# A four-layer graph network: layer 2 in units of up to three chunks, and the last group's tiles not cleared

## The chip, the cores and the metric

The kernel runs on one core of a Trainium2 chip. The metric is device time in microseconds. Before the change it is 1073.04 us, the median of three runs (1072.29 to 1073.3).

## The reference

There are 3327 nodes with 512 features, and a sparse adjacency matrix of 3327 x 3327 integers with some four neighbours a row. Four layers follow each other, each with a layer norm and a ReLU ahead and a residual around it:

```python
h = jnp.maximum(_layernorm(x, axis=-1), 0.0)
x = x + _L0_gnn_ref(h, adj, ...)   # mean over neighbours, two projections, a third on both, ReLU
h = jnp.maximum(_layernorm(x, axis=-1), 0.0)
x = x + _L1_gnn_ref(h, adj, ...)   # graph attention, 8 heads of 64
h = jnp.maximum(_layernorm(x, axis=-1), 0.0)
x = x + _L2_gnn_ref(h, adj, ...)   # graph attention, 4 heads of 128, quaternion weights, ELU
h = jnp.maximum(_layernorm(x, axis=-1), 0.0)
x = x + _L3_gnn_ref(h, adj, ...)   # graph attention, 1 head of 512
```

An attention layer projects every node to `Wh`, scores each edge by `leaky_relu(f_src[i] + f_dst[j])`, takes the softmax over the neighbours of a node, and sums the neighbours' `Wh` rows with those weights.

## The kernel before

The nodes are padded by one to 3328 and cut into 26 chunks of 128 rows. Everything that a layer needs of other nodes it gathers by index.

A first stage reads `adj` and `x`. For each chunk, `look` (L1189) loads two halves of the adjacency rows as integer tiles `ai` (four buffers) through `bring_rows` (L1182). VectorE finds the places of ones (`max_index`, L1209) and ScalarE counts them (L1217). The last chunk, number 25, has 127 rows, so `start` (L1197) clears the tile with a GpSimd memset (L1200) before its load, and `start_x` (L1289) clears its `x` tile with a VectorE memset (L1292). The loads of a chunk are issued on SyncE's queue, in the order in which the program emits them, and one that waits for a cleared tile holds those behind it. The same stage computes layer 0's projections on TensorE (L1349), makes the neighbour lists, and sorts the nodes by degree. Each node's row is then scattered to its sorted place in `own` (L1435).

After the sort, chunk 0 holds the nodes of highest degree. A chunk has as many slots as its largest degree can be: chunks 0 to 25 have 14, 8, 7, 7, 6, 6, 6, 5, 5, 5, 5, then five chunks of 4 (11 to 15), five of 3 (16 to 20), three of 2 (21 to 23) and two of 1. That makes 117 gathers a layer. One gather is an indirect DMA on GpSimd's queue (L1562): 128 rows of about 2 KB from the layer's `table` in DRAM into one of 33 places of the tile `ring`. `gather` (L1545) gives a chunk consecutive places, and starts from place 0 where the rest does not hold it. A place is written again once the chunk that held it has been read.

A layer's work on a chunk (`attend`, L1911) is: gather the slots; scores, softmax and weights on VectorE and ScalarE (L1941 to L1978), once for all chunks of a *unit*; scale the rows by the weights (VectorE L2110, ScalarE L2096 for one row in five); sum them in PSUM on TensorE with an identity matrix (`sum_on_pe`, L1593); in layer 2 the ELU, with the tiles `neg` and `ee` (L2164, L2166); add to the residual `xres` (L2178). Then `project` (L1602) makes the next layer's table: statistics for each chunk (L1649), the inverse deviation for the unit at once (`rough` L818, `refined` L827), ReLU, four transposes, a copy with sums, the products with the next layer's weights (L1737 for layer 3), and a store to the table on SyncE's queue (L1764). In layer 3 the weighted rows are summed on VectorE into a tile `y` (L2030), which TensorE transposes (L2046) and multiplies (L2060).

No layer's gather may start before the whole table is written: the `mark` memset (L2194) on GpSimd waits for all its stores.

The order of all this comes from `Plan` (L614). Every step is added with an engine, a cost and a rank, and with what it takes and gives of the limited buffers (`limits`, L1524). `Plan.run` (L650) goes through a schedule in which the step that can start first goes first, ties by rank, and emits the steps in that order; so a unit's place in `ORDERS` (L578) sets its rank, and its size and the number of buffers shape the order of instructions on every engine. Costs of the memsets are not among the plan's.

Of the kernel before, what the change touches and what calls it, by code (L numbers as in the profile page):

```python
# [8 lines left out]
F32 = mybir.dt.float32  # L9
# [9 lines left out]
P = 128  # L19
# [7 lines left out]
def general_path(  # L27
# [519 lines left out]
    def l3_finish(pc, i, o):  # L547
# [37 lines left out]
        (8, 13), (6,), (1,), (0,), (3,), (25,),  # L585
    ),
    2: (
        (18, 23), (19, 24), (16,), (20,), (6, 11), (10, 14), (7, 12), (5, 13), (9,), (1,), (21, 22), (4,), (0,),
        (8,), (2,), (3,), (15,), (17,), (25,),
    ),  # L590
    3: (
        (0,), (7,), (17,), (15, 20), (25,), (11,), (3,), (23,), (1, 5), (24,), (4, 14), (16,), (12, 22), (8,),
# [100 lines left out]
def gnn_stack_kernel(  # L693
# [19 lines left out]
    nc = tc.nc  # L713
    N, D = x_in.shape
    NK = (N + P - 1) // P
    NP = NK * P
    LAST = N - (NK - 1) * P
# [17 lines left out]
    with ExitStack() as st:  # L735
# [82 lines left out]
        def rough(pool, tag, var, scale=1.0):  # L818

            n = var.shape[-1]  # L820
            ln = pool.tile([P, 2], F32, tag="ln", name=f"ln{tag}", bufs=3)[:, :n]
            nc.scalar.activation(ln, var, AF.Ln, bias=eps, scale=scale)
            r0 = pool.tile([P, 2], F32, tag="r0", name=f"r0{tag}", bufs=3)[:, :n]
            nc.scalar.activation(r0, ln, AF.Exp, bias=lift, scale=-0.5)
            return r0

        def refined(pool, tag, mv, r0):  # L827

            n = r0.shape[-1]
            a = pool.tile([P, 2], F32, tag="nra", name=f"nra{tag}", bufs=3)[:, :n]  # L830
            nc.vector.scalar_tensor_tensor(a, r0, -1.0, r0, ALU.mult, ALU.mult)
            nc.vector.scalar_tensor_tensor(a, mv[:, :, 1], EPS, a, ALU.add, ALU.mult)
            r = pool.tile([P, 2], F32, tag="rs", name=f"rs{tag}", bufs=3)[:, :n]
            nc.vector.scalar_tensor_tensor(r, a, 3.0 * LIFT * LIFT, r0, ALU.add, ALU.mult)
            nmr = pool.tile([P, 2], F32, tag="nmr", name=f"nmr{tag}", bufs=3)[:, :n]
            nc.vector.scalar_tensor_tensor(nmr, mv[:, :, 0], -1.0, r, ALU.mult, ALU.mult)
            return r, nmr

        def refined_sums(pool, tag, mv, r0):

            n = r0.shape[-1]
            a = pool.tile([P, 2], F32, tag="nra", name=f"nra{tag}", bufs=3)[:, :n]
            nc.vector.scalar_tensor_tensor(a, r0, -1.0 / D, r0, ALU.mult, ALU.mult)
            nc.vector.scalar_tensor_tensor(a, mv[:, :, 1], D * EPS, a, ALU.add, ALU.mult)
            r = pool.tile([P, 2], F32, tag="rs", name=f"rs{tag}", bufs=3)[:, :n]
            nc.vector.scalar_tensor_tensor(r, a, 3.0 * LIFT * LIFT, r0, ALU.add, ALU.mult)
            nmr = pool.tile([P, 2], F32, tag="nmr", name=f"nmr{tag}", bufs=3)[:, :n]
            nc.vector.tensor_tensor(nmr, mv[:, :, 0], r, ALU.mult)
            return r, nmr


        with tc.tile_pool(name="p0", bufs=1) as pa, tc.tile_pool(name="p0p", bufs=2, space=PSUM) as pp:
# [329 lines left out]
            def bring_rows(dst, src, i):  # L1182
                if i < NK - 1:
                    nc.sync.dma_start(dst, src[i * P : (i + 1) * P, :])
                else:
                    nc.sync.dma_start(dst[:cut, :], src[i * P : i * P + cut, :])
                    nc.sync.dma_start(dst[cut:LAST, :], src[i * P + cut : N, :])

            def look(pos, i):  # L1189

                found = []
                rank = (ADJ * pos, 0)
                for hf in range(2):
                    key = f"{i}_{hf}"
                    cols = min(HW, N - hf * HW)

                    def start(i=i, hf=hf, key=key, cols=cols):  # L1197
                        ai = new("ai", key, [P, HW], I32)
                        if i == NK - 1:
                            nc.gpsimd.memset(ai, 0)  # L1200
                        bring_rows(ai[:, :cols], adj[:, hf * HW : hf * HW + cols], i)

                    o = load(rank, 4.0 * P * HW, start, take=("ai",), lag=1.6)

                    def find(i=i, hf=hf, key=key, cols=cols):
                        ai = tiles["ai", key]
                        for q in range(SEG // 2):
                            qq = hf * (SEG // 2) + q
                            nc.vector.max_index(  # L1209
                                fidx[:, i, qq * 8 : (qq + 1) * 8], one_i, ai[:, q * QW : min(cols, (q + 1) * QW)]  # L1210
                            )

                    a = put("dve", 2.06, rank, find, (), [o])

                    def square(i=i, hf=hf, key=key, cols=cols):
                        junk = pa.tile([P, HW], I8, tag="junk", name=f"junk{key}")
                        nc.scalar.activation(  # L1217
                            junk[:, :cols], tiles["ai", key][:, :cols], AF.Square, accum_out=sq[:, i, hf : hf + 1]
                        )

                    b = put("act", 1.8, rank, square, (), [o])
                    plan.add("none", 0.0, rank, None, [a, b], give=("ai",))
                    found.append(a)
                return found
# [63 lines left out]

            def start_x(i):  # L1289
                x = node(i)[:, :D]  # L1290
                if i == NK - 1:
                    nc.vector.memset(x, 0.0)  # L1292
                bring_rows(x, x_in, i)

            own_done = {}
# [220 lines left out]
        with tc.tile_pool(name="run", bufs=1, reuse_waits="tile") as pr, tc.tile_pool(  # L1516
# [4 lines left out]
            hsum = {  # L1521
                layer: pr.tile([P, NK, DC], F32, tag=f"hsum{layer}", name=f"hsum{layer}") for layer in (1, 2, 3)
            }
            limits = {"xy": 3, "acc": 2, "pt": 2, "pw": 2, "h": 3, "hT": 3, "t": 3, "neg": 2, "ee": 2, "y": 3}  # L1524
            limits.update({"norm": 2, "soft": 2, "w": 3, "mv": 3})
            plan = Plan(limits)
            tiles = {}
# [74 lines left out]
            def project(layer, unit, updated, rank):  # L1602
# [6 lines left out]
                n = len(unit)  # L1609
                norm = {}  # L1610
                seen = []
                if SUMMED[layer]:


                    def emit():
                        m = tiles["mv", (layer, unit[0])]
                        nc.vector.tensor_scalar(m[:, :n, 0], m[:, :n, 0], -1.0 / D, None, ALU.mult)

                    centred = plan.add("dve", 0.17, rank, emit, updated)
                    for j, i in enumerate(unit):  # L1620
# [12 lines left out]

                    guessed = plan.add("act", 0.6, rank, emit, seen)

                    def emit():
                        norm["r"], norm["nmr"] = refined_sums(
                            pr, f"{layer}_{unit[0]}", tiles["mv", (layer, unit[0])][:, :n, :], norm["r0"]
                        )

                    normed = plan.add("dve", 0.8, rank, emit, [guessed], take=("norm",), give=("mv",))
                else:
                    for j, i in enumerate(unit):

                        def emit(j=j, i=i):
                            if j == 0:
                                norm["mv"] = new("mv", (layer, unit[0]), [P, 2, 2])
                            st6 = pr.tile([P, 6], F32, tag="st6", name=f"st6_{layer}_{i}", bufs=2)
                            nc.vector.bn_stats(st6, xres[:, i, :])  # L1649
                            nc.vector.bn_aggr(norm["mv"][:, j, :], st6)  # L1650

                        seen.append(
                            plan.add("dve", 0.88, rank, emit, [updated[j]] + seen, take=("mv",) if j == 0 else ())
                        )

                    def emit():
                        norm["r0"] = rough(pr, f"{layer}_{unit[0]}", norm["mv"][:, :n, 1])

                    guessed = plan.add("act", 0.6, rank, emit, seen)

                    def emit():
                        norm["r"], norm["nmr"] = refined(
                            pr, f"{layer}_{unit[0]}", norm["mv"][:, :n, :], norm["r0"]
                        )

                    normed = plan.add("dve", 0.8, rank, emit, [guessed], take=("norm",), give=("mv",))
# [169 lines left out]
            def summing(layer, unit, j):  # L1836

                if not SUMMED[layer]:
                    return {}
                if j == 0:  # L1840
                    new("mv", (layer, unit[0]), [P, 2, 2])
                return {"accum_out": tiles["mv", (layer, unit[0])][:, j, 0:1]}


# [415 lines left out]
```

## Time and profile before

| | us |
|---|---|
| median of the runs | 1073.04 |
| the profiled execution's own time | 1231.77 |
| its span | 1230.0 |
| first stage and layer 0, to the first mark | 514.2 |
| layer 1, mark to mark | 245.3 |
| layer 2, mark to mark | 239.0 |
| layer 3, to the end | 231.5 |

The mean granted TensorE clock was 0.855 of full speed. Over the span TensorE was busy 901.8 us, VectorE 726.6, ScalarE 518.2 and GpSimd 610.1. In layer 2 they were busy 172.0, 151.5, 110.6 and 134.1 us. The profiled execution took 158.7 us longer than the median run, so its spans serve for proportions and for the durations of instructions, and differences of stages are compared only between profiles. In the views PE is TensorE, PEld its weight loads, DVE VectorE, ACT ScalarE, POOL GpSimd and SP SyncE; a `q` behind a name is that engine's sequencer. A timeline line has the start, the time taken, the engine, the line of the kernel, the operation, what it writes and reads, and in brackets the idle time before it and what ended it. "issue" and "remote" there name no instruction of another engine that was waited for.

### The profile page before, as it was taken

How to read it: one execution, taken by the hardware profiler on the slowest of the kernel's cores; microseconds unless marked ns; L12 is line 12 of the kernel's file. 1: busy time of each engine (PE TensorE's matmuls, PEld its weight loads, DVE VectorE, ACT ScalarE, POOL GpSimd, SP SyncE). 2: the span in 40 equal slices, each digit the busy share in tenths (PEclk: the TensorE clock that was granted, in tenths of full speed). 3: DMA queues.
4: the chain of work that ended last, by engine and by line, in shares of the span. 5: the costliest groups of instructions: out<-in, count | busy, mean ns of one | idle time of the engine just before them, and what ended most of it. 6: DMA issues, size and time to landing. Idle time of an engine off the chain costs nothing. (4 is left out here: it accounts for less than half of the span.)

```text
span 1230.0 us, 11605 instructions
## 1 busy us (share of the span) xinstructions
PE 901.8 (73%) x2853; PEld 510.4 (41%) x2853; DVE 726.6 (59%) x1848; ACT 518.2 (42%) x1700; POOL 610.1 (50%) x719
## 2 busy tenths in 40 slices
PE   7599999854098889752979796539979832948865
PEld 4244444322075656531647464214435421423322
DVE  6499989204176557453869784628894815534441
ACT  4488886210043433422656553316554621312221
POOL 1064246717655550175757511766883236675661
PEclk9899999977599899966989889659896956978987
DMA  9999894958587772265666521665754345575561
GB/s 352 338 364 338 294 306 146 317 203 286 172 268 252 247 249 89 76 195 149 198 183 178 154 79 55 189 187 150 209 169 129 91 121 149 168 206 160 163 186 59
DMA packets 89910, 240.49 MB, mean 196 GB/s; under 512 B 24933, under 2 KB 26477, under 8 KB 89834
## 3 DMA queue, kind: packets, MB, share of 16 engines
q0 software_dynamic: 41600, 137.72, 38.1%
q1 hardware_dynamic: 48234, 101.96, 23.3%
q8 instruction: 24, 0.39, 0.1%
q14 instruction: 52, 0.43, 0.1%
HBM read 190.35 MB, written 49.27 MB: 195 GB/s over the span
## 5 line engine op out<-in xcount | busy, mean ns | idle before, releaser
L1562 POOL DMA_INDIRECT ring<-table,nbr x351 | 368.5, 1050 | 185.5 <-issue 80.9
L1593 PE MATMUL acc<-ring,ident 128*128 128x512 f32 (+1 forms) x494 | 266.6, 676 | 66.8 <-DVE ring L2110 24.3
L1780 PE MATMUL pw<-w,hT 128*128 128x264 f32 (+1 forms) x832 | 197.3, 394 | 18.3 <-ACT hT L1705 13.6
L1780 PEld LDWEIGHTS pw<-w,hT 128*128 128x128 f32 x832 | 161.2, 195 | 60.9 <-ACT hT L1705 20.5
L1593 PEld LDWEIGHTS acc<-ring,ident 128*128 128x128 f32 (+1 forms) x494 | 98.7, 215 | 175.1 <-issue 107.5
L1562 POOL DMA_INDIRECT ring<-table,srec x117 | 110.1, 941 | 77.8 <-issue 31.5
L2110 DVE TENSOR_TENSOR ring<-ring,w 128x2048 f32<-128x2048 f32 (+7 forms) x76 | 114.3, 1531 | 4.7 <-DVE w L1978 3.0
L2060 PE MATMUL pw<-w,hT 128*128 128x512 f32 x208 | 101.7, 634 | 13.3 <-ACT hT L2052 11.0
L1209 DVE FIND_INDEX8 fidx<-one_i,ai 128x8 uint32<-128x832 int32 x104 | 104.2, 1018 | 0.0
L1349 PE MATMUL pz_n<-wf,hT_n 128*128 128x512 f32 x208 | 95.2, 609 | 10.9 <-ACT hT_n L1342 8.4
L1705 ACT ACTIVATE hT<-pt 128x128 f32<-128x128 f32 (+1 forms) x312 | 81.8, 292 | 39.7 <-PE pt L1694 18.5
L1217 ACT ACTIVATE junk<-ai 128x1664 int8<-128x1664 int32 (+1 forms) x52 | 82.7, 1590 | 32.6 <-DMA ai<-in_adj_dram 32.2
L1694 PE MATMUL pt<-ident,h 128*128 128x128 f32 x208 | 36.5, 312 | 75.9 <-ACT h L1676 73.4
L1349 PE MATMUL py_n<-wf,hT_n 128*128 128x512 f32 x208 | 91.9, 592 | 0.0
L1803 ACT COPY t<-pw 128x512 f32<-128x512 f32 (+1 forms) x54 | 30.6, 566 | 134.0 <-PE pw L1780 43.9
L1941 DVE TENSOR_TENSOR e<-ring,fs 128x24 f32<-128x24 f32 (+25 forms) x96 | 15.2, 172 | 120.2 <-DMA ring<-table,nbr 102.0
L2060 PEld LDWEIGHTS pw<-w,hT 128*128 128x128 f32 x208 | 42.3, 207 | 73.2 <-issue 51.3
L1705 ACT ACTIVATION_READ_ACCUMULATOR hT<-pt 128x1 f32 x312 | 69.5, 223 | 0.0
L1694 PEld LDWEIGHTS pt<-ident,h 128*128 128x128 f32 x208 | 28.1, 160 | 96.3 <-ACT h L1676 81.6
L2194 POOL MEMSET mark<- 1x1 f32 x3 | 0.3, 88 | 132.7 <-DMA table<-t 132.7
L1349 PEld LDWEIGHTS pz_n<-wf,hT_n 128*128 128x128 f32 x208 | 39.8, 195 | 62.8 <-issue 49.4
L2046 PE MATMUL pt<-ident,y 128*128 128x128 f32 x96 | 16.4, 312 | 67.4 <-issue 56.8
(185 smaller groups left out, 1319.7 us busy)
## 6 DMA issues: line engine op xcount, KB each, us to landing
ai<-in_adj_dram SPq DMA_DIRECT2D x25, 832.0 KB
ai<-in_adj_dram SPq DMA_DIRECT2D x25, 831.5 KB
table<-t SPq DMA_DIRECT2D x52, 258.0 KB
xy<-own SPq DMA_DIRECT2D x26, 512.0 KB
table<-t SPq DMA_DIRECT2D x26, 260.0 KB
table<-zt_n SPq DMA_DIRECT2D x26, 256.0 KB
ring<-table,nbr POOLq DMA_INDIRECT x351
later<-in_x_dram SPq DMA_DIRECT2D x15, 256.0 KB
```

Of the source, the lines that this page charges most:

```text
L1209: nc.vector.max_index(fidx[:, i, qq * 8 : (qq + 1) * 8], one_i, ai[:, q * QW : min(cols, (q + 1) * QW)])
L1217: nc.scalar.activation(junk[:, :cols], tiles["ai", key][:, :cols], AF.Square, accum_out=sq[:, i, hf : hf + 1])
L1349: nc.tensor.matmul(pz, tiles["hT", key][:, c, :], wf[s][:, c, :], start=(c == 0), stop=(c == DC - 1))
L1562: nc.gpsimd.indirect_dma_start(out=ring[:m, r0 + s, : width[layer]], out_offset=None, in_=table[layer], in_offset=bass.IndirectOffsetOnAxi ...
L1593: nc.tensor.matmul(acc, ident[:m, :], g[:m, s, :D], start=(k == 0), stop=(k == len(slots) - 1))
L1694: nc.tensor.transpose(pt[:, c, :], h[:, c * P : (c + 1) * P], ident)
L1705: nc.scalar.activation(hT[:, c, :n], pt[:, c, :n], AF.Copy, accum_out=hsum[layer][:, i, c : c + 1])
L1780: nc.tensor.matmul(pw[:, b, :w], tiles["hT", key][:, c, :], wsb[layer][:, c, b, :w], start=(c == 0), stop=(c == DC - 1),)
L1803: nc.scalar.copy(t[:, :D].rearrange("p (b f) -> p b f", b=2)[:, lo:hi, :], pw[:, lo:hi, :HD])
L2046: nc.tensor.transpose(pt[:, c, :], tiles["y", key][:, c * P : (c + 1) * P], ident)
L2060: nc.tensor.matmul(pw[:, 0, :], tiles["hT", key][:, c, :], w3[:, c, :], start=False, stop=(c == DC - 1))
L2110: nc.vector.tensor_tensor(v, v, box["w"][:m, j, lo:hi, :].unsqueeze(3).to_broadcast([m, hi - lo, H, O]), ALU.mult,)
```

## The change

Layer 2's 26 chunks are taken in 18 units instead of 19, in another order; two units have three chunks, where the largest had two. The small tiles that hold one value per chunk of a unit are three wide instead of two. Of the tiles `neg` and `y` there is one buffer less each. The adjacency and feature tiles of the last chunk are no longer cleared: `bring_rows` loads the last real row once more into the one padding row, a third DMA for each of the three tiles. Later steps leave the padding node out by `real` (L781) and by the bounds of the output's scatter, as they did.

```diff
     2: (
-        (18, 23), (19, 24), (16,), (20,), (6, 11), (10, 14), (7, 12), (5, 13), (9,), (1,), (21, 22), (4,), (0,),
-        (8,), (2,), (3,), (15,), (17,), (25,),
+        (21,), (16, 24), (22,), (9, 17, 19), (12,), (2,), (23,), (11, 14), (15, 20), (5,), (4, 7, 13), (6, 8),
+        (0,), (1,), (3,), (18,), (10,), (25,),
     ),
...
-            ln = pool.tile([P, 2], F32, tag="ln", name=f"ln{tag}", bufs=3)[:, :n]
+            ln = pool.tile([P, 3], F32, tag="ln", name=f"ln{tag}", bufs=3)[:, :n]
...
                     nc.sync.dma_start(dst[:cut, :], src[i * P : i * P + cut, :])
                     nc.sync.dma_start(dst[cut:LAST, :], src[i * P + cut : N, :])
 
+                    nc.sync.dma_start(dst[LAST:P, :], src[N - 1 : N, :])
+
...
                         ai = new("ai", key, [P, HW], I32)
-                        if i == NK - 1:
-                            nc.gpsimd.memset(ai, 0)
                         bring_rows(ai[:, :cols], adj[:, hf * HW : hf * HW + cols], i)
...
                 x = node(i)[:, :D]
-                if i == NK - 1:
-                    nc.vector.memset(x, 0.0)
                 bring_rows(x, x_in, i)
...
-            limits = {"xy": 3, "acc": 2, "pt": 2, "pw": 2, "h": 3, "hT": 3, "t": 3, "neg": 2, "ee": 2, "y": 3}
+            limits = {"xy": 3, "acc": 2, "pt": 2, "pw": 2, "h": 3, "hT": 3, "t": 3, "neg": 1, "ee": 2, "y": 2}
...
-                                norm["mv"] = new("mv", (layer, unit[0]), [P, 2, 2])
+                                norm["mv"] = new("mv", (layer, unit[0]), [P, 3, 2])
```

The other tiles of `rough`, `refined` and `refined_sums` and the other `mv` change in the same way as `ln` and `mv`.

More of the change, by code (lines that the diff above doesn't have):

```diff
@@ L820, in rough @@
             n = var.shape[-1]
-            ln = pool.tile([P, 2], F32, tag="ln", name=f"ln{tag}", bufs=3)[:, :n]
+            ln = pool.tile([P, 3], F32, tag="ln", name=f"ln{tag}", bufs=3)[:, :n]
             nc.scalar.activation(ln, var, AF.Ln, bias=eps, scale=scale)
-            r0 = pool.tile([P, 2], F32, tag="r0", name=f"r0{tag}", bufs=3)[:, :n]
+            r0 = pool.tile([P, 3], F32, tag="r0", name=f"r0{tag}", bufs=3)[:, :n]
             nc.scalar.activation(r0, ln, AF.Exp, bias=lift, scale=-0.5)
@@ L829, in refined @@
             n = r0.shape[-1]
-            a = pool.tile([P, 2], F32, tag="nra", name=f"nra{tag}", bufs=3)[:, :n]
+            a = pool.tile([P, 3], F32, tag="nra", name=f"nra{tag}", bufs=3)[:, :n]
             nc.vector.scalar_tensor_tensor(a, r0, -1.0, r0, ALU.mult, ALU.mult)
             nc.vector.scalar_tensor_tensor(a, mv[:, :, 1], EPS, a, ALU.add, ALU.mult)
-            r = pool.tile([P, 2], F32, tag="rs", name=f"rs{tag}", bufs=3)[:, :n]
+            r = pool.tile([P, 3], F32, tag="rs", name=f"rs{tag}", bufs=3)[:, :n]
             nc.vector.scalar_tensor_tensor(r, a, 3.0 * LIFT * LIFT, r0, ALU.add, ALU.mult)
-            nmr = pool.tile([P, 2], F32, tag="nmr", name=f"nmr{tag}", bufs=3)[:, :n]
+            nmr = pool.tile([P, 3], F32, tag="nmr", name=f"nmr{tag}", bufs=3)[:, :n]
             nc.vector.scalar_tensor_tensor(nmr, mv[:, :, 0], -1.0, r, ALU.mult, ALU.mult)
@@ L841, in refined_sums @@
             n = r0.shape[-1]
-            a = pool.tile([P, 2], F32, tag="nra", name=f"nra{tag}", bufs=3)[:, :n]
+            a = pool.tile([P, 3], F32, tag="nra", name=f"nra{tag}", bufs=3)[:, :n]
             nc.vector.scalar_tensor_tensor(a, r0, -1.0 / D, r0, ALU.mult, ALU.mult)
             nc.vector.scalar_tensor_tensor(a, mv[:, :, 1], D * EPS, a, ALU.add, ALU.mult)
-            r = pool.tile([P, 2], F32, tag="rs", name=f"rs{tag}", bufs=3)[:, :n]
+            r = pool.tile([P, 3], F32, tag="rs", name=f"rs{tag}", bufs=3)[:, :n]
             nc.vector.scalar_tensor_tensor(r, a, 3.0 * LIFT * LIFT, r0, ALU.add, ALU.mult)
-            nmr = pool.tile([P, 2], F32, tag="nmr", name=f"nmr{tag}", bufs=3)[:, :n]
+            nmr = pool.tile([P, 3], F32, tag="nmr", name=f"nmr{tag}", bufs=3)[:, :n]
             nc.vector.tensor_tensor(nmr, mv[:, :, 0], r, ALU.mult)
@@ L1840, in summing @@
                 if j == 0:
-                    new("mv", (layer, unit[0]), [P, 2, 2])
+                    new("mv", (layer, unit[0]), [P, 3, 2])
                 return {"accum_out": tiles["mv", (layer, unit[0])][:, j, 0:1]}
```

## The prediction

> **What bounds the kernel now.** I read the span and clock first, then the busy time by stage, the waits inside layer 2, the timelines of the engines there, and last the stretch in which the last group of nodes is loaded. The stages are cut where the three `mark` memsets (L2194) run, which wait for every table row of a layer to be written: 514.2, 759.5 and 998.5 us. Layer 2, the one that is reordered, is 239.0 of the span's 1230.0 us. By stretches (columns: stretch, length, busy us and instruction count of PE, PEld, DVE, ACT, POOL, granted clock, DMA share, GB/s):
>
> ```profile
> 780.00:800.00 20.00, 12.37 (x37) 7.20 (x37) 13.07 (x35) 9.09 (x30) 15.68 (x15) 0.76 0.66 183
> 800.00:820.00 20.00, 3.68 (x6) 1.20 (x4) 4.06 (x17) 0.71 (x4) 14.14 (x15) 0.59 0.74 210
> ...
> 860.00:880.00 20.00, 19.03 (x61) 9.60 (x60) 17.03 (x37) 11.33 (x40) 16.14 (x13) 0.91 0.70 195
> ...
> 940.00:960.00 20.00, 20.00 (x47) 9.21 (x46) 10.02 (x24) 7.26 (x29) 7.38 (x8) 0.74 0.29 82
> 960.00:980.00 20.00, 19.04 (x68) 9.66 (x67) 18.30 (x48) 11.75 (x47) 1.08 (x2) 1.00 0.23 77
> ```
>
> No engine bounds the layer alone. POOL issues gathers until 961; PE and DVE are over 85% busy at 860 to 880, PE is full at 940 to 980, and near 800 to 820 all stand still. The gathers, from the POOL timeline:
>
> ```profile
> 932.84 0.95 POOL L1562 DMA_INDIRECT ring<-table,nbr  x1 [0.30 <-issue]
> 934.09 0.95 POOL L1562 DMA_INDIRECT ring<-table,nbr  x1 [0.30 <-DVE nra L831]
> 950.00 0.92 POOL L1562 DMA_INDIRECT ring<-table,nbr  x1 [14.96 <-PE acc L1593]
> ```
>
> One gather each 1.25 us; the 109th (chunk 3's last row) waits 15 us for ring place 18, which chunk 0 holds until PE has summed it. PE was full through that wait, so it cost little. After the last gather at 960.4 it takes 38 us to the mark.
>
> The start, and the place where clearing acts:
>
> ```profile
> 770.10 0.17 DVE L1941 TENSOR_TENSOR e<-ring,fs 128x12 f32<-128x12 f32 x1 [15.76 <-DMA ring<-table,nbr]
> 772.52 0.20 DVE L1941 TENSOR_TENSOR e<-ring,fs 128x8 f32<-128x8 f32 x1 [2.24 <-DMA ring<-table,nbr]
> 776.14 1.22 PE L1593 MATMUL acc<-ring,ident 128*128 128x512 f32 x1 [16.47 <-DVE ring L2110]
> ```
>
> ```profile
> 146.12 1.49 POOL L1200 MEMSET ai<- 128x1664 int32 x1 [23.36 <-DVE fidx L1209]
> 147.56 1.29 POOL L1131 TENSOR_TENSOR later<-w,later 128x512 f32<-128x512 f32 x1
> 148.78 1.50 POOL L1200 MEMSET ai<- 128x1664 int32 x1
> ```
>
> ```profile
> SPq L1186 <- POOL ai L1200: 10.3, 2, 9.0
> ```
>
> PE waits for the first gathers and the softmax; the SP queue stands 10.3 us behind the two clears, of which most is the wait for a free `ai` buffer, not the memset.
>
> **What the Trainium skill says.** Perfetto Trace Analysis, Sequencer Loop: a sequencer takes instructions one after the other and waits for their semaphores there. The trace agrees: the product behind the first clear (L1131) starts at 147.56, after 23 us of waiting. TensorE: Matmul & The Clock Gate, Part 1: PE at rest falls to half clock and is released by about 3.4 us of work. The trace agrees: 0.59 where PE was busy 3.7 of 20 us, 1.00 at 960 to 980. DMA: Bandwidth & Descriptors, Anatomy of one DMA: 2.0 us plus the bytes over 436e3 per us, an estimate of 2.6 us for a gather's 264 KB; here the third gather starts at 766.27 and is used at 770.10, 3.8 us, which I use.
>
> **The change part by part.**
>
> Clears. Removed are two POOL memsets (1.49 us each) and one DVE memset (0.49 us at 14.2, in an empty stretch). Added are three loads of one row, 0.33 to 0.44 us of SP each as its neighbours show. SP can start chunk 25's first half at 146.1 instead of 147.6 (-1.5) and the second at best 3.4 us earlier; the x loads and later `ai` loads behind follow. That helps DVE, whose waits there are 2.7 us (159.0) and 2.1 us (167.5). The cover is PE: its own-row products run almost without a gap from 119 to 235 and end at 267.7; only its 1.25 us wait for the sort at 214.3 can go. POOL is freed of 23 us, but its scatters start at 219.2 on DVE's sorted places. I take -1.3. Without PE's cover it would be -3.4; if the single-row load lands late, +1.
>
> Fewer units. 19 units become 18. One merge saves DVE six small softmax steps (0.18 to 0.20 us each, 1.1 with the gaps 1.3) and four refining steps (4 x 0.16, 0.6 with one rounding): -1.9 us of DVE, and about 0.9 of ACT.
>
> The order. I compare, at each unit, when its rows can be there plus the work still to do. Gathers cost 1.25 us each. PE: 0.95 us a row (rows in threes take 2.84) plus 1.5 a chunk (0.6 turning, 0.95 `v3`): 148 us in all. DVE: 2.3 a chunk (two updates 0.7 each, statistics 0.87), about 1.9 a unit, 0.55 a row not scaled by ACT: 157.5 before, 155.7 after.
>
> - Before: the first unit needs 5 gathers, 6.3 + 157.5 = 163.8 for DVE; chunk 0 comes at gather 90 with 48.5 of PE left, 112.5 + 48.5 = 161.0.
> - After: the first unit is chunk 21 with 2 gathers, 2.5 + 155.7 = 158.2 for DVE; units (9,17,19), 23.8 + 136.4 = 160.2; (4,7,13) end at gather 68 with 76.3 of PE left, 85 + 76.3 = 161.3; chunk 0 at gather 93, 116.3 + 44.1 = 160.4.
>
> The larger sum falls from 163.8 to 161.3: -2.5, the merge included. That PE starts 3.75 us sooner is real, but of it only this arrives.
>
> The ring. 33 places are given out in order, from 0 again where a chunk does not fit. Counting through, chunk 0 before took places 18 to 31 from chunks 13, 5 and 9, read long ago: at least 24 gathers lie between. After it takes 0 to 13 from chunk 4, 7 and 13, which are one unit that is complete only at gather 68; place 0 is wanted at gather 80, twelve later, 15.0 us. Chunk 4 needs 3.8 (landing) + 2.6 (scores, exponential, weights) + 2.3 (product) + 5.7 (six rows on PE) = 14.4. So it fits with nothing queued, and every us of queue in front becomes a stall of POOL. Behind that gather stand all later ones; the last row of chunk 0 then comes 14 x 1.25 + 8.7 = 26.2 us after chunk 4 is read. PE's cover is chunks 7, 13, 6, 8: 20 rows x 0.95 + five chunks x 1.5 = 26.5. Just enough: I take +1.0, bounds 0 and +10 (4 us of PE rest, then the half clock for some 10 us). In exchange chunk 0's places are wanted next at gather 112 (19 on, as before), with 6 gathers behind instead of 9: nothing, as PE was full.
>
> Buffers. `neg` 2 to 1: writer and reader are both ACT, which go one after the other already (0.60, then 0.63): 0. A three-chunk unit takes all three `t` tiles at once; two such units only: 0 to +2. `y` 3 to 2 in layer 3: freed by four transposes; PE is busy 140.4 of 231.5 us there and covers; if it is behind by one chunk (5.2 us of PE) the DVE waits: 0 to +5. Taken together +0.4. Wider small tiles cost nothing: the views have the same n.
>
> Tail. Last before 25 is chunk 10 (five rows) for 17 (three): up to 1.9 us of PE and 1.2 of DVE later; the sums at that place (gather 116) are 3 to 5 us under the largest, so 0.
>
> Sum: -1.3 - 2.5 + 1.0 + 0.4 = -2.4 against the profiled 1231.8 (span 1230.0). The median of the runs shown, 1073.0, is 158.7 lower: instruction times carry over, but stalls with no releaser, such as 794 to 823, need not be there. Without them the layer keeps nearer to the sums, and DVE's own largest sum, which falls from 163.8 to 160.2 (-3.6), shows more. I take -3.5: 1069.5.
>
> **Rivals.** *Nothing moves:* POOL makes 117 gathers of the same bytes in either order, 146 us, and the barriers stay. For: DMA share 0.7. Against: the layer is 93 us longer than that. Gives 1072. *Chunk 0 starves PE:* the twelve-gather distance. For: in the trace rows wait 30 to 45 us between the unit's last gather and its `neg` (unit 5, 13: 847 to 882), so the ring is full. Against: then PE has queued work. It decides once PE runs dry over 3 us before chunk 0; price +8, 1081. *The gathers run freely:* the 15 us wait goes and the drain starts earlier. Against: PE was full in it. If half counts, -8: 1064.
>
> **How the numbers follow.** Forecast 0.42, of which 0.03 ends less than 2.1 us off; gathers free 0.14; nothing moves 0.12; starved 0.32. 0.2%, 2.1 us, is about what a measurement of this kernel tells from no change. So faster 0.53, same 0.15, slower 0.32. The range takes the free case's far side (1058) and the starved one (1081); the likeliest alone is 1066 to 1071.
>
> **What would show it.** No L1200 memset and SP at chunk 25's half near 146. First PE sum 12 to 13 us after layer 2's mark instead of 16.7. No ring wait over 5 us before chunk 0's gathers; a long one followed by PE idle and half clock means the rival. Mark to mark under 239. Layer 3 the same to 2 us; more would come from `y`. Wrong, too, if stalls without releaser move with the order.

## The result and the profile after

The changed kernel takes 1079.51 us (median of 12 runs, 1074.17 to 1085.63) beside 1073.26 us (12 runs, 1072.29 to 1079.43) for the kernel before on the same chip: ratio 1.0052, 95% interval 1.0037 to 1.0067. By this ratio it is slower by 5.6 us (the medians lie 6.3 us apart), where 3.5 us faster was forecast.

The profile of before that the prediction read came from an execution of 1231.8 us. Profiled again, the kernel before took 1076.75 us, and the profiled execution of after 1076.58. These two are comparable, and from here on "before" is the second profile. The two executions took the same time although the medians differ, so this pair doesn't contain the whole loss; where it lies is read from all profiles of the two orders. The line numbers of kernels without the clears are two lower from L1200 on.

By stages (us from the span's start, read at the first gather of each layer; the first three rows have the same order of instructions in layer 2, the last two the new one):

| | layer 0 | layer 1 | layer 2 | layer 3 | end | layer 2 | layer 3 |
|---|---|---|---|---|---|---|---|
| before, again | 268.1 | 451.3 | 655.2 | 870.1 | 1074.6 | 214.9 | 204.5 |
| clears removed only | 268.1 | 452.2 | 657.1 | 869.9 | 1076.0 | 212.8 | 206.1 |
| fewer buffers only | 267.9 | 451.9 | 655.8 | 866.4 | 1069.4 | 210.6 | 203.0 |
| after | 265.4 | 449.1 | 654.4 | 871.1 | 1074.8 | 216.7 | 203.7 |
| new order, smaller buffers, clears kept | 269.0 | 452.2 | 656.4 | 874.5 | 1078.2 | 218.1 | 203.7 |

Layer 2, from first gather to first gather, is 212.8 us on average in the old order (210.6 to 214.9) and 217.4 in the new one (216.7 and 218.1): 4.6 us, most of the loss. From mark to mark the layer seems to shrink, 218.2 to 213.6 us, but that cut misleads: after the mark, layer 3's first gather still waits for the last store of the table, 0.8 us before and 7.5 us after. So the mark doesn't stand for the whole table being written, as was said ahead of the prediction.

Layer 2 by stretches, before (columns as in the prediction: length, then busy us of PE, PEld, DVE, ACT and POOL, the granted clock, DMA share, GB/s). The last stretch ends where TensorE begins the last row of the layer's last sum:

```profile
655.20:675.20 20.00, 7.57 (x10) 2.90 (x10) 7.97 (x21) 1.66 (x4) 15.69 (x15) 0.57 0.64 175
675.20:715.20 40.00, 32.60 (x112) 18.61 (x113) 33.03 (x89) 24.89 (x99) 31.77 (x28) 0.83 0.72 202
...
795.20:849.40 54.20, 53.03 (x145) 26.41 (x144) 40.42 (x96) 27.31 (x110) 28.94 (x23) 0.81 0.51 145
sum 194.20, PE 161.01 PEld 84.76 DVE 143.91 ACT 98.47 POOL 140.25; mean PE 32.20 PEld 16.95 DVE 28.78 ACT 19.69 POOL 28.05
```

The same of after:

```profile
654.40:674.40 20.00, 9.54 (x14) 3.44 (x14) 10.15 (x30) 4.77 (x11) 15.41 (x16) 0.58 0.65 186
674.40:714.40 40.00, 26.78 (x79) 14.72 (x78) 28.88 (x66) 18.11 (x71) 31.47 (x29) 0.74 0.75 214
...
794.40:850.40 56.00, 51.57 (x167) 26.25 (x166) 41.56 (x101) 31.13 (x126) 27.36 (x23) 0.88 0.42 124
sum 196.00, PE 156.92 PEld 80.99 DVE 144.48 ACT 99.28 POOL 135.86; mean PE 31.38 PEld 16.20 DVE 28.90 ACT 19.86 POOL 27.17
```

TensorE is 2 us better off in the first 20 us and 5.8 us worse off in the next 40. Its idle time up to the last sum (194.20 - 161.01 = 33.2 us before) is 39.1 us after. The last sum begins at 196.0 us, and at 197.5 with the new order and the clears kept, against 192.5 on average in the three runs of the old order. What follows the last sum is the same: 20.7 us in both. VectorE's busy time did not shrink (150.7 us before and 150.9 after over the layer).

The start, which went as forecast. PE's first sum before, and DVE's first scores and PE's first sum after:

```profile
667.62 7.57 PE L1593 MATMUL acc<-ring,ident 128*128 128x512 f32 x10 [16.32 <-DVE ring L2110]
```

```profile
659.29 0.17 DVE L1939 TENSOR_TENSOR e<-ring,fs 128x8 f32<-128x8 f32 x1 [14.21 <-DMA ring<-table,nbr]
662.22 3.78 PE L1591 MATMUL acc<-ring,ident 128*128 128x512 f32 x4 [11.81 <-DVE ring L2108]
```

The first sum is 12.2 us after the mark (650.0) instead of 16.5. By the first unit of three the gain is gone. PE, ACT and DVE of after, where the first unit of three, (9, 17, 19), comes in; some lines between are left out:

```profile
679.50 3.78 PE L1591 MATMUL acc<-ring,ident 128*128 128x512 f32 x4 [2.37 <-DVE ring L2108]
...
682.85 0.17 DVE L1939 TENSOR_TENSOR e<-ring,fs 128x12 f32<-128x12 f32 x1 [2.35 <-DMA ring<-table,nbr]
683.07 1.91 PE L1692 MATMUL pt<-ident,t 128*128 128x128 f32 x8
...
686.19 0.65 ACT L2162 ACTIVATE neg<-acc 128x512 f32<-128x512 f32 x1
...
687.53 0.70 DVE L2170 SCALAR_TENSOR_TENSOR acc<-acc,ee 128x512 f32<-128x512 f32 x1 [3.67 <-ACT ee L2164]
...
690.60 2.29 DVE L2108 TENSOR_TENSOR ring<-ring,w 128x2048 f32<-128x2048 f32 x1
...
692.95 5.49 PE L1591 MATMUL acc<-ring,ident 128*128 128x512 f32 x6 [6.16 <-DVE ring L2108]
```

PE had little to do with four small chunks, and the granted clock is low (0.59 from 674.4 to 694.4 us); its sum of chunk 22 ends at 683.28. The ELU of that sum (L2162) stands on ACT behind eight copies of turned tiles and starts at 686.19; DVE's update waits for it, and the product of the next unit stands behind the update. PE is idle for 6.16 us.

PE also runs dry just before chunk 0's first sum in after, as it does, again for 3.85 us, with the new order and the clears kept. In the three profiles of the old order no gap directly before chunk 0's sum is over 1.5 us:

```profile
806.69 5.10 PE L1591 MATMUL acc<-ring,ident 128*128 128x512 f32 x6 [3.85 <-DVE ring L2108]
```

The waits of POOL for a place of the ring, after (the gathers 80 and 112 of the layer), and the only one over 1 us before (gather 109). For gather 80 the view names no releaser; that it waits for a place which chunk 4 held is inferred from the count of places:

```profile
773.23 0.94 POOL L1560 DMA_INDIRECT ring<-table,nbr  x1 [3.14 <-issue]
...
826.23 0.94 POOL L1560 DMA_INDIRECT ring<-table,nbr  x1 [6.47 <-PE acc L1591]
```

```profile
820.43 0.91 POOL L1562 DMA_INDIRECT ring<-table,nbr  x1 [2.08 <-PE acc L1593]
```

The clears, in the waits of the SP queue, before and after:

```profile
SPq L1186 <- POOL ai L1200: 8.6, 2, 7.4
```

```profile
SPq L1186 <- DVE fidx L1209: 7.8, 2, 7.5
```

The queue waits nearly as long as before, now for VectorE to release the buffer: the memset was little of what it stood for.

### The profile page after: what moved, and what is told of

Its sections match the earlier page's. It is cut to its first block, busy times and chain, and to the rows that moved or that the text cites. A ratio compares the mean times of both kernels' runs of the same rounds, so it can differ in the third digit from the quotient of the medians.

```text
span 1074.8 us, 11569 instructions
## 1 busy us (share of the span) xinstructions
PE 873.9 (81%) x2853; PEld 495.0 (46%) x2853; DVE 725.6 (68%) x1837; ACT 518.4 (48%) x1697; POOL 614.2 (57%) x717
## 5 line engine op out<-in xcount | busy, mean ns | idle before, releaser
L1560 POOL DMA_INDIRECT ring<-table,nbr x351 | 375.6, 1070 | 131.4 <-issue 62.3
L1591 PE MATMUL acc<-ring,ident 128*128 128x512 f32 (+1 forms) x494 | 258.6, 660 | 83.4 <-DVE ring L2108 55.5
L1778 PE MATMUL pw<-w,hT 128*128 128x264 f32 (+1 forms) x832 | 193.2, 389 | 2.9 <-ACT hT L1703 2.9
L1591 PEld LDWEIGHTS acc<-ring,ident 128*128 128x128 f32 (+1 forms) x494 | 95.1, 207 | 189.3 <-issue 78.8
L2108 DVE TENSOR_TENSOR ring<-ring,w 128x2048 f32<-128x2048 f32 (+7 forms) x76 | 114.5, 1533 | 1.6
L1939 DVE TENSOR_TENSOR e<-ring,fs 128x16 f32<-128x16 f32 (+23 forms) x96 | 15.2, 171 | 123.1 <-DMA ring<-table,nbr 111.3
L1347 PE MATMUL pz_n<-wf,hT_n 128*128 128x512 f32 x208 | 92.3, 595 | 0.9 <-ACT hT_n L1340 0.8
L822 ACT ACTIVATE ln<-mv,eps 128x1 f32<-128x1 f32 (+2 forms) x59 | 17.8, 301 | 104.0 <-DVE mv L1648 96.8
L2094 ACT ACTIVATE ring<-ring,w 128x64 f32<-128x64 f32 (+1 forms) x216 | 57.7, 360 | 4.2 <-DVE w L1976 3.1
L2028 DVE SCALAR_TENSOR_TENSOR acc<-ring,w,acc 128x512 f32<-128x512 f32 (+2 forms) x67 | 50.5, 754 | 13.6 <-ACT acc L2026 12.0
L1966 ACT ACTIVATE ex<-el 128x48 f32<-128x48 f32 (+21 forms) x55 | 12.5, 235 | 96.0 <-DVE el L1949 96.0
```

Source lines behind the costliest of these rows:

```text
L1347: nc.tensor.matmul(pz, tiles["hT", key][:, c, :], wf[s][:, c, :], start=(c == 0), stop=(c == DC - 1))
L1560: nc.gpsimd.indirect_dma_start(out=ring[:m, r0 + s, : width[layer]], out_offset=None, in_=table[layer], in_offset=bass.IndirectOffsetOnAxi ...
L1591: nc.tensor.matmul(acc, ident[:m, :], g[:m, s, :D], start=(k == 0), stop=(k == len(slots) - 1))
L1778: nc.tensor.matmul(pw[:, b, :w], tiles["hT", key][:, c, :], wsb[layer][:, c, b, :w], start=(c == 0), stop=(c == DC - 1),)
L2028: nc.vector.scalar_tensor_tensor(to[:m, :], row, weight, acc[:m, :], ALU.mult, ALU.add)
L2094: nc.scalar.activation(v, v, AF.Copy, scale=box["w"][:m, j, s, h : h + 1])
```

## The experiments

**Which part of the change: theories A (the order of layer 2), B (clears and one-row loads), C (one `y` less).** Four kernels on one chip, where before had 1075.26 us (54 runs). The kernel before as it is:

> The kernel before, unchanged, for a second profile of it and for the noise of the comparison. Every theory: ratio 1.000 within 0.2%. The first profile of it took 1231.8 us against runs of 1073; if that is one odd execution, this profile should be near 1075 with layer 2 (mark to mark) near 205 us; the changed kernel's profile has 213.6 there.

Measured: 1.0005 (0.9991 to 1.0018). Then the edits of `bring_rows`, `start` and `start_x` alone:

> Only the clears of the last group's tiles go, and the third one-row load comes in; order and buffers are as before. Theory A (the order of layer 2 makes the loss): 1072 us, ratio 0.998 to 1.001. Theory B (the one-row loads make it): 1077 to 1079, ratio 1.004 to 1.006, and the first mark several us later.

Measured: 1.0014 (1.0000 to 1.0028), and layer 0's first gather at 268.1 us as without the edit. No gain, and at most a small loss. In layer 2 the order of instructions is that of before. The buffers alone:

```diff
-            limits = {..., "neg": 2, "ee": 2, "y": 3}
+            limits = {..., "neg": 1, "ee": 2, "y": 2}
```

> Only neg goes from 2 buffers to 1 and y from 3 to 2; order and clears are as before. Theory A: 1073 us, ratio 0.999 to 1.001. Theory C (one y less makes layer 3 slower): 1077 to 1079, ratio 1.004 to 1.006, with layer 3 some 4 us longer and layer 2 unchanged.

Measured: 0.9970 (0.9945 to 0.9994). The order of instructions is the same on every engine as before, and layer 3 takes 203.0 us beside 204.5. So nothing is lost with `y`, and two builds with the same order of instructions may lie 0.3% apart. A single ratio within 0.3% of another is therefore not taken as a difference below; the loss of 0.5% is not twice that, and rests on two builds, after and the next. The order of layer 2 with the wider tiles and the buffers, clears kept:

> The new order of layer 2 with the three-wide tiles and the smaller limits, but with the clears kept. Theory A: 1078 to 1080 us, ratio 1.004 to 1.007. Theory B: 1073 us, ratio 1.000. Theory C: as A, but with layer 2 no longer than before and layer 3 longer.

Measured: 1.0053 (1.0034 to 1.0072), the loss of the whole change. A holds, B and C fall. This kernel has the wider small tiles too; that they are not the cause is shown further down by h3, which differs from the changed kernel in layer 2's order alone and measures 1.0001.

**Why the order: theories A1 (the two ring waits) and A2 (a unit of three releases no row to TensorE before its last row is there).** The four kernels first ran on a chip where the kernel before took 1224.01 us (11 runs, 1192.18 to 1232.23):

```diff
f1  -(9, 17, 19),        +(9,), (17,), (19,),
f2  f1, and -(4, 7, 13), +(4,), (7,), (13,),
f3  -(6, 8), (0,), (1,), (3,), (18,), (10,), (25,)
    +(6, 8), (10,), (0,), (1,), (3,), (18,), (25,)
f4  f2 and f3 together
```

> The changed kernel with the unit (9, 17, 19) of layer 2 taken as three units of one chunk; (4, 7, 13) stays a unit. Theory A1, the two ring waits of GpSimd (gather 80 behind chunk 4, 3 us; gather 112 behind chunk 0, 6.5 us) make the loss: the distances of 12 and 19 gathers are as they were, so the ratio to the kernel before stays at 1.004 to 1.006 and layer 2 from its first gather to layer 3's first gather stays at about 217 us. Theory A2, a unit of three holds its gathered rows back from TensorE until its last row is there: a good half of the loss goes, ratio 1.001 to 1.003, about 214 us, and TensorE is idle less than the 9 us it was idle in the 40 us from 690 on.

> The changed kernel with both units of three taken apart, six units of one chunk in the same order. A1: gather 80 now has 21 gathers between the last row of chunk 4 and itself and no longer waits, gather 112 does as before; of the loss 3 us at most goes, ratio 1.003 to 1.005, 215 us. A2: all of the loss goes, ratio 0.999 to 1.001, 212 to 213 us.

> The changed kernel with chunk 10 of layer 2 taken ahead of chunk 0 instead of near the end, so that no gather of the layer wants chunk 0's places again; both units of three stay. A1: the 6.5 us wait at gather 112 goes and at most 3 us of ring waits stay; ratio 0.998 to 1.002, 211 to 214 us. A2: little moves, ratio 1.004 to 1.006, 216 to 218 us.

> The changed kernel with both edits, the two units of three taken apart and chunk 10 ahead of chunk 0. Both A1 and A2: the whole loss goes, ratio 0.996 to 1.001, 210 to 213 us, no ring wait above 2 us in layer 2. If it stays at 1.004 or more, the loss comes from neither, but from something else in the order, such as chunks 0, 1 and 3 lying next to each other near the end.

Measured there: 1235.42, 1235.30, 1235.73 and 1231.74 us, all 0.6 to 1.0% above the kernel before, with nothing to tell them apart. All layers but the first stage were longer on that chip, by stand-stills like these of ACT in f1, which wait for no instruction that the profile names:

```profile
789.79 0.28 ACT L1703 ACTIVATE hT<-pt 128x128 f32<-128x128 f32 x1 [15.13 <-remote]
...
799.60 0.28 ACT L1703 ACTIVATE hT<-pt 128x128 f32<-128x128 f32 x1 [8.67 <-remote]
```

They decide neither A1 nor A2. f2 and f3 were run once more on another chip (before 1077.02 us, 25 runs):

> The same kernel as before under this edit (both units of three of layer 2 taken apart, six units of one chunk in the same order), on another chip, since on the last one the kernel before itself took 1224 us with stand-stills that no instruction explains. Theory A1 (the ring waits at gathers 80 and 112 make the loss): gather 80 no longer waits, gather 112 does; ratio 1.003 to 1.005. Theory A2 (a unit of three holds its rows back from TensorE): the whole loss goes, ratio 0.999 to 1.001, and from the layer's first gather to layer 3's first gather 212 to 213 us.

> The same kernel as before under this edit (chunk 10 of layer 2 ahead of chunk 0, units of three kept), on another chip than the last. A1: the 6.5 us wait of gather 112 goes; ratio 0.998 to 1.002, 211 to 214 us from first gather to first gather. A2: little moves, ratio 1.004 to 1.006, 216 to 218 us.

Measured: taken apart, 1.0150 (1.0121 to 1.0180), and 228.4 us from first gather to first gather. Without the late ring wait, 1.0045 (1.0027 to 1.0063). A1 falls in both (in the first, gather 80 still waited 5.7 us). A2 falls with the first, though its ratio held in the second. The sums of layer 2, after and with the units taken apart:

```profile
sum 216.70, PE 167.47 PEld 89.64 DVE 150.93 ACT 110.27 POOL 135.95; mean PE 167.47 PEld 89.64 DVE 150.93 ACT 110.27 POOL 135.95
```

```profile
sum 228.40, PE 173.78 PEld 93.86 DVE 155.33 ACT 113.10 POOL 138.75; mean PE 173.78 PEld 93.86 DVE 155.33 ACT 113.10 POOL 138.75
```

Four units more cost VectorE 4.4 us, 1.1 a unit, and the layer 11.7: with these chunks in this order the units of three are a gain. The other edit doesn't take the ring wait away alone: it puts chunk 10's five gathers ahead of chunk 0, whose last row is issued 145.0 us after the layer's first gather instead of 137.4. Its profile, an execution 5.6 us above the median, has 224.0 us for the layer. POOL's longest ring wait is 1.25 us there, and a new wait has come; DVE and PE:

```profile
762.40 0.18 DVE L1939 TENSOR_TENSOR e<-ring,fs 128x16 f32<-128x16 f32 x1 [6.55 <-DMA ring<-table,nbr]
...
768.66 2.07 PE L1591 MATMUL acc<-ring,ident 128*128 128x512 f32 x2 [11.67 <-DVE ring L2108]
```

VectorE stands 6.55 us at the scores of (4, 7, 13), whose last rows are not there, with the update and the product of the unit before it queued behind; TensorE runs dry.

**Where in the order: theories B1 (the opening) and B2 (middle and end).** Before had 1077.09 us (43 runs).

```diff
h1  +(18, 23), (19, 24), (16,), (20,), (6, 11), (21, 22), (9, 17), (12,), (2,), (14, 15), (5,), (4, 7, 13),
    +(8,), (0,), (1,), (3,), (10,), (25,),
h2  +(21,), (16, 24), (22,), (9, 17, 19), (18, 23), (20,), (6, 11), (10, 14), (7, 12), (5, 13), (1,), (4,),
    +(0,), (8,), (2,), (3,), (15,), (25,),
```

> The changed kernel with layer 2's first five units taken from the kernel before ((18, 23), (19, 24), (16,), (20,), (6, 11)) and the rest in the order of the change, as far as the chunks that are left allow; (4, 7, 13) stays a unit and the ring distance of gather 89 is 12 again. Both earlier theories have fallen: without the units of three the kernel was slower still, without the ring waits no faster. Theory B1, the opening makes the loss: in the 20 to 60 us after the layer's first gather TensorE was busy 32.6, 32.6 and 34.1 us in three runs of the old order and 26.8 to 27.5 us in four of the new; with the old opening it is 32 to 34 us again, and the ratio to the kernel before comes to 0.998 to 1.002, 212 to 214 us from first gather to first gather. Theory B2, the middle and the end of the order make it (the unit of three at the places of chunk 0, chunks 0, 1 and 3 together near the end): ratio 1.004 to 1.008, 217 us.

> The changed kernel with only layer 2's first four units ((21,), (16, 24), (22,), (9, 17, 19)) of the change and after them the order of the kernel before. B1: TensorE busy 26.5 to 28 us in the 20 to 60 us after the first gather, ratio 1.004 to 1.007, 216 to 219 us. B2: ratio 0.998 to 1.002, 212 to 214 us, whatever the opening does.

Measured: 1.0016 (1.0000 to 1.0032) and 1.0012 (0.9993 to 1.0030). TensorE's busy time in the 20 to 60 us followed the opening exactly, 34.1 us and 27.9, but the times did not: neither half makes the loss, and the two losses together are about half of it. With the old opening POOL even waited 10.33 us at gather 112, longer than in after, at a third of its loss:

```profile
830.46 0.95 POOL L1560 DMA_INDIRECT ring<-table,nbr  x1 [10.33 <-PE acc L1591]
```

**Do TensorE's idle times add: theories C1 (they do) and C2 (what is won in one stretch is lost in another).** Before had 1075.50 us (35 runs).

```diff
i1  h1 with  -(8,), (0,), (1,), (3,), (10,), (25,)   +(8,), (10,), (0,), (1,), (3,), (25,)
i2  h2 with  -(0,), (8,), (2,), (3,), (15,), (25,)   +(15,), (0,), (8,), (2,), (3,), (25,)
h3  the old order with (21, 22) moved to the front
```

> The old opening with the rest of the changed order (the last experiment but one) and chunk 10 ahead of chunk 0, so that gather 112 does not wait for chunk 0. TensorE's idle time from the layer's first gather to its last sum is the measure: 33 to 35 us in the old order, 39 to 41 in the new; with the old opening 36.2, of which 8.9 us after the 140th us, where GpSimd waited 10 us for chunk 0's place. Theory C1, TensorE's idle time in the opening and at the late ring wait add up: the late idle falls to 3 to 5 us, the sum to 31 to 33 us, ratio 0.996 to 0.999. Theory C2, losses of place do not add, whatever is won in one stretch is lost in a later one: idle sum 35 us or more, ratio 1.000 to 1.003.

> The new opening with the rest of the old order (the last experiment) and chunk 15 ahead of chunk 0, so that only the last chunk's one gather wants a place of chunk 0. In the run without this edit TensorE was idle 22.7 us in the first 60 us (old order 19.4, new 23.7) and 11.4 us after the 140th, with a ring wait of 6.1 us at gather 113. C1: the opening stays at 22 to 24 us, the late idle falls to 3 to 5 us, the sum to 32 to 34 us, ratio 0.996 to 1.000. C2: idle sum 37 us or more, ratio 1.001 to 1.005.

> The kernel before's order with one unit moved: (21, 22), four rows, to the very front, with the other parts of the change kept. It gives TensorE its first sum as early as the change does without the change's later units. C1: the first 20 us have 1.5 to 2 us less idle time, the 40 us after them as before (6 to 7.5 us); the rest shifts little; ratio 0.997 to 1.000. C2: ratio 1.000 to 1.004, with the idle time coming back later.

Measured: 1.0071 (1.0045 to 1.0098), 1.0031 (1.0015 to 1.0047), 1.0001 (0.9981 to 1.0020). i1 took the ring wait away as meant, but like g3 it issues chunk 0's last row later (148.7 us after the first gather, 141.6 in h1), and it is slower than h1 by some 6 us (0.55%). ACT, DVE and PE of i1 before chunk 0's first sum:

```profile
814.50 0.26 ACT L1966 ACTIVATE ex<-el 128x56 f32<-128x56 f32 x1
820.26 0.19 DVE L1939 TENSOR_TENSOR e<-ring,fs 128x28 f32<-128x28 f32 x1 [8.82 <-DMA ring<-table,nbr]
...
827.36 4.56 PE L1591 MATMUL acc<-ring,ident 128*128 128x512 f32 x6 [11.59 <-DVE ring L2108]
```

Chunk 0's exponentials (56 = 14 slots of 4 heads) are ready at 814.8, but next on VectorE's queue are the scores of chunk 1 (28 = 7 of 4), whose last row lands at 820. And h3, whose first sum came only 1.8 us earlier, has TensorE idle 13.9 of the first 20 us and 14.2 us in the 20 to 60 us, more than any kernel with the new opening on these chips, and 39.9 us up to the last sum, as much as after (39.1); its median loses nothing. (Its profile is of an execution 2.7 us above that median, with 216.3 us for the layer.) So the idle time of one profile doesn't fix the median to such differences. C1 falls; C2 gave the range for i2 and h3, and i1 is outside both.

**Theory D (head-of-line waiting, that is, ready work standing behind an instruction that waits for a late row, since the planner has gathers at 1.27 us and they take 1.5) and E (the units' order sets the time).** Before had 1073.50 us (11 runs). The kernels leave units and buffers as they are:

```diff
-                    issue = plan.add("pool", pool_cost(held(i, s)), rank, emit, after)
+                    issue = plan.add("pool", 1.5 if layer == 2 else pool_cost(held(i, s)), rank, emit, after)
```

> The changed kernel, with only the planner's cost of a layer 2 gather set to 1.5 us instead of 1.27; units, order of units and buffers stay, but the planner emits each engine's instructions in another order. Measured, the 117 gathers of the layer take 175 to 178 us from first to last, 1.5 us each. Theory D, the loss is head-of-line waiting: VectorE, ScalarE and TensorE take their instructions in the emitted order, which was made for gathers that come at 1.27 us, so VectorE stands at the scores of a unit whose last row is late while ready work stands behind it (6.6 us in one run and 8.8 us in another, after each of which TensorE was idle 11.6 us), and each order of units pays a different sum of such waits. With the right pace these waits shrink: at most one wait of VectorE for gathered rows above 3 us after the first, ratio to the kernel before 0.993 to 1.001. Theory E, the order of units itself sets the time: ratio 1.004 to 1.007 as without the edit.

> The kernel before with only the planner's cost of a layer 2 gather set to 1.5 us. D: VectorE's waits for gathered rows, 20 us a layer after the first one with one of 6 and one of 5 us, fall to half; ratio 0.990 to 0.999, and before and after come within 3 us of each other. E: 0.998 to 1.003.

> The kernel before with the planner's gather cost set to what the layers measured: 1.27, 1.4, 1.5 and 1.5 us for layers 0 to 3. D: layers 1 and 3 gain as well, each 0 to 4 us; ratio 0.985 to 0.998. E: 0.997 to 1.004, as layers 1 and 3 have been the same in all runs.

Measured: the changed kernel with it 1.0252 (1.0220 to 1.0285), the kernel before with it 1.0104 (1.0074 to 1.0134), all layers 1.0199 (1.0167 to 1.0230), there with layer 3 at 219.4 us from its first gather to the end. Neither theory gave such a loss. The waits of layer 2 (us in total, times, longest), before, and before with the new pace:

```profile
DVE e L1941 <- DMA ring<-table,nbr: 35.3, 8, 15.6
...
DVE acc L2172 <- ACT ee L2166: 16.6, 10, 4.9
```

```profile
DVE acc L2172 <- ACT ee L2166: 28.3, 14, 6.8
...
DVE e L1941 <- DMA ring<-table,nbr: 17.8, 2, 15.7
```

The waits for rows did what D said, 19.7 us beside the first one to 2.1; but VectorE, which now takes scores later, waits 11.7 us more for ACT's ELU, which follows PE's sums, and 12 us more for the exponentials. In the changed kernel the sum of that ELU wait grows from 19.9 us to 45.3. There GpSimd also waits 9.7 us at gather 78 and 8.1 at gather 80, so in that kernel the new pace tests more than late rows:

```profile
DVE acc L2170 <- ACT ee L2164: 19.9, 12, 3.7
```

```profile
DVE acc L2170 <- ACT ee L2164: 45.3, 11, 13.6
```

No kernel here beats the one before by more than the 0.3% by which two builds with equal orders differ.

## Why the prediction was wrong

**Clears, -1.3.** SP did start chunk 25's first half at the time worked out, 146.2 us. Nothing came of it: alone, the edit left layer 0's first gather at 268.1 us, and on the chips where before takes 1073 to 1077 us that gather comes at 267.4 us on average in ten profiles without the clears and 267.7 in five with them. The cover, TensorE's own-row products, was named, but -1.3 was booked as if it could leak; nothing of it is seen.

**Fewer units, -1.9 of VectorE.** The ten instructions did go (374 to 364 in the layer), but their summed length fell by 1.0 us, 158.4 to 157.4, since the steps of the units of three are longer. Instructions overlap a little at their ends, and the busy time, which counts that once, is 150.7, 150.8 and 150.9 us in the three runs of the old order, 150.9 and 150.7 in the new: nothing saved. A unit costs 1.1 us of VectorE by the run that added four, not 1.9.

**The order, -2.5: the step that failed.** The first sum came at 12.2 us, as forecast. But the sums "arrival plus the work still to do" had two terms wrong, and each alone takes the gain away.

The first is VectorE's work. The 157.5 us is near the summed length of its instructions; busy it was 151.5 us in the profile that the prediction read, and 150.7 in the second one. With 151.5 the first unit before gives 157.8, not 163.8. Then TensorE's sums are the largest on both sides, 161.0 and 161.3, and no gain is left. The step from -2.4 to -3.5 leaned on the same 163.8.

The second is the arrivals. A gather was booked at 1.25 us; from the layer's first to its last one they take 1.48 to 1.56 us each in these five profiles. Chunk 3's last row before (gather 109, shown above) was issued 165.2 us after the first, where 1.25 us each gives 135. Chunk 10's last row after (gather 116) was issued 177.3 us after the first, where 1.25 us each gives 144:

```profile
831.68 0.91 POOL L1560 DMA_INDIRECT ring<-table,nbr  x1 [0.30 <-issue]
```

An estimate with the prediction's own work terms and these arrivals: the largest sum of TensorE is 180.5 to 185.4 us in the three profiles of the old order, all at chunk 3, and 185.9 and 187.8 in the two of the new, both at chunk 10. On average that is 3.9 us more, where 2.5 less was forecast; VectorE's largest sum grows by some 2 us. The last sum on TensorE was 4.2 us later (192.5 and 196.8). By this estimate the late rows decide this pair, and not the opening that the prediction compared. The same estimate doesn't rank the other orders: it gives h1 188.9 at a ratio of 1.0016 and i1 183.2 at 1.0071.

What it leaves out are the links between the engines, since it takes each engine as working without a gap once its rows are there. A row passes scores, exponential, product, sum, ELU, update and turning on three engines that each take their instructions in the emitted order; in i1 VectorE stood 8.8 us at chunk 1's scores with chunk 0's weights behind. What the Trainium skill says in Perfetto Trace Analysis, Sequencer Loop, that a sequencer's instructions wait for their semaphores, was the right thing to use (the trace of i1 agrees, with these 8.8 us); it was applied to SP and not to VectorE.

**The ring, +1.0.** Gather 80 waited 3.1 us, more than booked and within the bounds. Gather 112 was booked at nothing "as PE was full" and waited 6.5 us; it is among the late arrivals above. What it costs alone no run shows: the two edits that removed it put chunk 0 later, and with a wait of 10.3 us another order lost less.

**Buffers +0.4, tail 0, layer 3 the same.** Buffers and layer 3 hold as far as one profile can tell: buffers alone show no loss, and layer 3 differs by 0.8 us. The tail was put at 0 because the sums at gather 116 lie under the largest; with the measured arrivals that of chunk 10, at this gather, is the largest after. The time behind the last sum is 20.7 us in both.

**Rivals and signs.** The starved TensorE gave the right sign and nearly the time (1081), and its sign was met, 3.9 us of rest before chunk 0. That its price fits is luck: h2 has 10.3 us of rest at the same place and measures 1.0012. "Mark to mark under 239" was a bad sign to choose: it came true (213.6) while the layer grew. The doubt on the stand-still at 794 to 823 was right: in the second profile PE is busy 19.0 of the matching 20 us (691.4 to 711.4), which held 3.7.

**What stays open.** Shown is that layer 2's order makes the loss, and that neither the units of three nor the opening makes it alone. That the loss comes through late rows and a later last sum on TensorE is read from five profiles, not tested by a run that changes this alone. Which property of an order makes it good is not found: with units untouched, the emitted order alone moved the time by 1 to 2%, two to four times what the change did.

## What to carry to other kernels

Where several engines take their instructions in an order written by a planner, counting arrivals and remaining work per engine did not rank orders that differ by a few us. If you count, take the arrivals from their measured pace over the whole layer and not from an undisturbed stretch, and take busy time and not summed lengths. Then read the idle time of the busiest engine stretch by stretch and ask what stood in front of the ready work on the engine before it. An edit that takes a wait away moves other work too: here each one meant to remove a wait (for ring places, late rows, joined units) was no faster or cost time. Check first that the profile's own time agrees with the median, and cut stages at the first work of the next stage, not at a marker.

## What the runs showed of the hardware

- The same program took 1224 us on one chip and 1073 to 1077 us on four others, with stand-stills of 9 to 15 us that wait for nothing named.
- The four matmuls that sum two rows took 3.78 us at 679.50 us in after, in a stretch at a granted clock of 0.59, and 1.88 us at 698.87 us, in a stretch at 0.89: in the thin opening a row costs TensorE double. The Trainium skill (TensorE: Matmul & The Clock Gate, Part 1) says that PE at rest falls to half clock; this trace agrees.
- A gather's issue on GpSimd takes 0.95 us as a rule and up to 2.8 in some (ns, min/median/max, layer 2 of after and the first gathers of layer 3):

```profile
L1560 POOL DMA_INDIRECT ring<-table,nbr x121: 867/946/2816, 654.4 to 874.9; - x121
```

- The long ones begin while VectorE scales rows. In layer 2 of after, 29 of the 117 gathers began during a product of L2108, and 25 of these took over 1.05 us; of the other 88 one did. Before it is 23 of 28 and 1 of 89. Nearly all of the long ones end 0.8 us after the product does, as this one, after the product of 690.60 shown above, which ends at 692.89:

```profile
691.81 1.90 POOL L1560 DMA_INDIRECT ring<-table,nbr  x1 [0.30 <-issue]
```

- These stretched issues add some 25 us to the layer's gathers (117 at 0.95 us are 111 us, and GpSimd was busy 136). If the products cause them, the pace of the gathers depends on the order itself. No run moved the products away to test it.
